# A graph-attention layer: most of the output stage placed between the last edge steps, joined rows loaded in one piece, and a node stage with paired statistics and half its rows on GpSimd

## Chip, core and metric

The kernel runs on one core of a Trainium2 chip. The core has a matrix engine (PE, with a separate record of its weight loads, PEld), a vector engine (DVE), an activation engine (ACT), GpSimd (POOL) and SyncE (SP); SP, ACT and POOL also issue DMAs, and 16 DMA engines move the bytes. The metric is the device time of one execution in microseconds (us).

## What is computed

12,500 nodes with 128 features and 400,000 edges, sorted by target node:

```python
h = jnp.maximum(_layernorm(x), 0.0)
msg = (h @ w_src + b_src)[src] + (h @ w_dst)[dst]        # per edge
msg = msg * edge_weight1 * radial_mlp(edge_attr_32)
msg_h = (msg @ w_sep + b_sep).reshape(E, 8, 32)          # 8 heads
alpha, value = smooth_leaky_relu(msg_h[:, :, :16]), msg_h[:, :, 16:]
att = segment_softmax(einsum(alpha, alpha_dot), dst)
out = segment_sum(value * att, dst).reshape(N, 128)
return x + out @ w_proj + b_proj
```

## The kernel before

**Node stage** (lines 157 to 433). The 12,500 rows are held as 98 tiles of 128 rows, worked on in 25 quads of four tiles. `stats` takes, for each tile on DVE, one batch-norm statistics and one aggregation instruction; `scales` turns them on ACT (square root) and DVE into `rstd` and `shift`; `norm` is four ACT instructions per quad (a ReLU with scale and bias); `turn` transposes the quad on PE and copies it back with DVE; `products` multiplies by `w_src` (k=0) and `w_dst` (k=1) on PE, copies with ACT, and SP stores the rows in the DRAM tables `t_src` and `t_dst`. The loop at line 407 writes the order out by hand: in turn i come the turning of quad i+1, the norm of quad i+3, the products of quad i, the statistics of quad i+5. At i=1 `load_targets` puts DMAs of single words on SP's queue; at i=6 `first` loads one block of source indices (`ri`) on SP and casts and transposes it; from i=3 on two weight loads are issued per turn; at i=13 `fits` computes `bad`, which picks this path or a fallback. `cuts` (line 361) comes last.

**Edge stage** (`windows`, line 747). 391 steps (`NP`), each for two sections of 512 edges. `gather` (line 856) issues 128-row indirect DMAs of `t_src` on POOL, eight per step. The values of a section are summed per target by `values`, `one_hot` and `sums`, 13 steps later (`LAG`), so that after the last gather 14 more steps drain (the loop at line 1353, j = 0 to 13). Each step's sums `ob` (three buffers) go by `store_win` to `win` and by `store` (line 1083) as two 63-row DMAs on SP to the rows of `agg` at an address read from a register. A section's first and last node are shared with its neighbours; those rows are joined in 13 blocks, whose results stand in `obs_d`, and `scatter` (line 1190) writes each block to `agg` with an indirect DMA on POOL. Before, the drain's step j loads one block into `comb` (two buffers, line 1359) and scatters it; a `store` of step c >= 384 is declared independent of the scatters, one below is not. The last two blocks are computed in the drain itself (`jobs`, lines 1341 to 1368).

**Output stage** (`final`, line 1387), after the drain. It loads `agg` in nine pieces of up to 12 tiles on SP (line 1396), divides by the softmax's sums (`quotients`, DVE), and then for each of 25 quads: `turn` (PE, copy on ACT), `finish` (product with `w_proj` on PE, addition of `x_fin` on DVE, store of `out` on SP, line 1434). `x_fin` is loaded on ACT in the drain. All of these tiles have 128 partitions, but for the last of 84 rows.

**Rows of 125.** One transfer of the kernel before has tiles of 125 partitions: `zero` (line 136) writes `z` (125 partitions of 680 values) over `agg`, 20 times, two per step, at the start of the edge stage.

Of the kernel before, what the change touches and what calls it, by code (L numbers as in the profile page):

```python
# [21 lines left out]
F32 = mybir.dt.float32  # L22
# [8 lines left out]
P = 128  # L31
C = 128
# [24 lines left out]
def gnn_kernel(ctx: ExitStack, tc: tile.TileContext, a: dict, out: bass.AP):  # L57
# [9 lines left out]
    NX = -(-NP // MP) * MP * PR  # L67
    assert NT * P == E and RC * RP == E and NT % TPI == 0 and NT % SORT_T == 0
# [88 lines left out]
    with tc.tile_pool(name="node", bufs=2) as np_, tc.tile_pool(name="node1", bufs=1) as n1, \  # L157
# [6 lines left out]
        for t0, t1 in groups:  # L164
            nc.sync.dma_start(out=x_all[:, t0:t1, :], in_=x_v[:, t0:t1, :])
        nc.sync.dma_start(out=x_all[:tail, NF, :], in_=x[NF * P:, :])
# [12 lines left out]
        ends = n1.tile([NH, 17, 2], I32, name="ends")  # L179
        eb = n1.tile([P, NS, 2], I32, name="eb")  # L180
# [6 lines left out]
        def load_targets():  # L187
# [3 lines left out]
            with nc.allow_non_contiguous_dma(reason="single targets"):  # L191
                nc.sync.dma_start(out=cur[1:P, 0:1], in_=bass.AP(at.tensor, at.offset, [[CC, P - 1], [1, 1]]))
                at = dst[0:1]
                h = NH - 1
                nc.sync.dma_start(out=ends[0:h], in_=bass.AP(
                    at.tensor, at.offset, [[34 * SEC // 2, h], [SEC, 17], [SEC - 1, 2]]))
# [28 lines left out]
        mv = n1.tile([P, NB, 2], F32, name="mv")  # L225
        nc.vector.memset(mv, 1.0)
# [3 lines left out]
        def stats(t0, t1):  # L230
            for t in range(t0, t1):
                n = rows(t)
                st = np_.tile([P, nc.vector.BN_STATS_DIM], F32, name="st", bufs=4)
                nc.vector.bn_stats(st[:n], x_all[:n, t, :])
                nc.vector.bn_aggr(mv[:n, t, :], st[:n])

        def scales(t0, t1):
            s = slice(t0, t1)
            nc.scalar.activation(rstd[:, s], mv[:, s, 1], AF.Sqrt, bias=eps, scale=1.0)
            nc.vector.reciprocal(rstd[:, s], rstd[:, s])  # L240
            nc.vector.scalar_tensor_tensor(shift[:, s], mv[:, s, 0], -1.0, rstd[:, s],
                                           op0=ALU.mult, op1=ALU.mult)

        def norm(i):
            t0, t1 = quads[i]
            hs[i] = np_.tile([P, 4, C], F32, name="h", bufs=4)
            for t in range(t0, t1):
                n = rows(t)
                nc.scalar.activation(hs[i][:n, t - t0, :], x_all[:n, t, :], AF.Relu,
                                     bias=shift[:n, t:t + 1], scale=rstd[:n, t:t + 1])  # L250

        def turn(i):
# [3 lines left out]
            for t in range(t0, t1):  # L256
# [3 lines left out]
            nc.vector.tensor_copy(x_all[:, t0:t1, :].rearrange("p u n -> p (u n)")[:, :w],  # L260
                                  pt.rearrange("p u n -> p (u n)")[:, :w])
# [44 lines left out]
        def fits():  # L306
# [14 lines left out]
            nc.vector.tensor_copy(bad, sum_)  # L321
# [425 lines left out]
    def windows():  # L747
# [7 lines left out]
        with tc.tile_pool(name="ps", bufs=1, space=PSUM) as pp, \  # L755
# [327 lines left out]
            def store(c, f):  # L1083
                at = nc.sync.value_load(base[0:1, f, c:c + 1])
                st = nc.sync.dma_start(out=agg[ds(at, W - 1), :], in_=accs[c][f * W:(f + 1) * W - 1, :])
                if 2 * c + 1 >= (NC - 1) * (P // 2):
                    tc.declare_no_dep(st.ins, group="combined", reason="its rows follow those of the blocks")
# [102 lines left out]
            def scatter(g):  # L1190
# [6 lines left out]
                tc.add_to_no_dep_group("combined", st.ins)  # L1197

            comb = {}

            def combined(g):
                comb[g] = tail_pool.tile([P, ROW], F32, name="comb", bufs=2)
                return comb[g]
# [128 lines left out]
            tail_pool = held.enter_context(tc.tile_pool(name="fin1", bufs=1, side="right"))  # L1332
            x_fin = tail_pool.tile([P, NB, C], F32, name="x_fin")
            x_loads = load_xb(x_fin)
            last = NC - 1

            def out_rows(g):
                block_rows_out(g, combined(g))
# [13 lines left out]
            assert SB * (NC - 1) + LAG + 1 == NP + 7  # L1352
            for k in range(NP, NP + LAG + 1):
# [9 lines left out]
            for _ in x_loads:  # L1363
                pass
# [5 lines left out]
            with tc.tile_pool(name="fin", bufs=3) as fp:  # L1370
                final(fp, x_fin, lambda i: pp.tile([P, 4, P], F32, name=("pm0", "pm1", "V")[i % 3]),
                      lambda i: pp.tile([P, 4, C], F32, name=("p3", "pa", "m1")[i % 3]))


    XQ = 12
    out_v = out[0:NF * P, :].rearrange("(p t) c -> p t c", t=NF)
    agg_v = agg[0:NF * P, :].rearrange("(p t) c -> p t c", t=NF)

    def load_xb(x_fin):

        for t0, t1 in groups:
            nc.scalar.dma_start(out=x_fin[:, t0:t1, :], in_=xb_v[:, t0:t1, :])
            yield
        nc.scalar.dma_start(out=x_fin[:tail, NF, :], in_=xb[NF * P:N, :])
        yield

    def final(fp, x_fin, turned, product):
        starts = list(range(0, NB, XQ))
        gs, qs, qTs = {}, {}, {}

        def load_g(i):

            gs[i] = fp.tile([P, XQ, ROW], F32, name="g", bufs=len(starts))
            for n, t0, t1 in blocks(starts[i], min(starts[i] + XQ, NB)):
                o = starts[i]
                nc.sync.dma_start(out=gs[i][:n, t0 - o:t1 - o, :],
                                  in_=agg_v[:, t0:t1, :] if n == P else agg[NF * P:N, :].unsqueeze(1))

        def quotients(i):
            r = fp.tile([P, XQ, H], F32, name="r")  # L1400
            qs[i] = fp.tile([P, XQ, C], F32, name="q")
            g = gs.pop(i)
            for n, t0, t1 in blocks(starts[i], min(starts[i] + XQ, NB)):
                s = slice(t0 - starts[i], t1 - starts[i])
                m = t1 - t0
                nc.vector.tensor_scalar(r[:n, s, :], g[:n, s, C:ROW], 1e-16, None, op0=ALU.add)  # L1406
                nc.vector.reciprocal(r[:n, s, :], r[:n, s, :])  # L1407
                nc.vector.tensor_mul(  # L1408
                    qs[i][:n, s, :].rearrange("p t (h k) -> p (t h) k", h=H),
                    g[:n, s, 0:C].rearrange("p t (h k) -> p t h k", h=H),  # L1410
                    r[:n, s, :].unsqueeze(3).to_broadcast([n, m, H, C // H]))

        def turn(i):
            t0, t1 = quads[i]
            q, o = qs[t0 // XQ], t0 // XQ * XQ
            pt = turned(i)
            for t in range(t0, t1):
                n = rows(t)
                nc.tensor.transpose(pt[:, t - t0, :n], q[:n, t - o, :], ident[:n, :n])  # L1419
            w = (t1 - t0 - 1) * P + rows(t1 - 1)  # L1420
            qTs[i] = fp.tile([P, 4, P], F32, name="qT")
            nc.scalar.copy(qTs[i].rearrange("p u n -> p (u n)")[:, :w], pt.rearrange("p u n -> p (u n)")[:, :w])

        def finish(i):
            t0, t1 = quads[i]
            qT = qTs.pop(i)
            py = product(i)
            for t in range(t0, t1):
                n = rows(t)
                nc.tensor.matmul(py[:n, t - t0, :], qT[:, t - t0, :n], w_proj, start=True, stop=True)  # L1430
            for n, u0, u1 in blocks(t0, t1):
                y = x_fin[:n, u0:u1, :]
                nc.vector.tensor_add(y, py[:n, u0 - t0:u1 - t0, :], y)  # L1433
                nc.sync.dma_start(out=out_v[:, u0:u1, :] if n == P else out[NF * P:N, :].unsqueeze(1), in_=y)

        for i in range(len(starts)):
            load_g(i)
        quotients(0)
        turn(0)
        for i in range(Q):  # L1440
            if i % 3 == 1 and i // 3 + 1 < len(starts):
                quotients(i // 3 + 1)
            if i + 1 < Q:
                turn(i + 1)
            finish(i)


# [3 lines left out]
    with fit.Else():  # L1451
# [23 lines left out]
        with tc.tile_pool(name="fin_b", bufs=3) as fp, tc.tile_pool(name="fin1_b", bufs=1) as f1, \  # L1475
                tc.tile_pool(name="fin_ps", bufs=2, space=PSUM) as fps, tc.manual_schedule():
            x_fin = f1.tile([P, NB, C], F32, name="x_fin")
            for _ in load_xb(x_fin):
                pass
            final(fp, x_fin, lambda i: fps.tile([P, 4, P], F32, name="pt"),  # L1480
                  lambda i: fps.tile([P, 4, C], F32, name="py"))
# [36 lines left out]
```

## Time and profile before

| | us |
|---|---|
| median of three runs (lowest, highest) | 4234.25 (4232.47, 4238.16) |
| the profiled execution | 4228.57 |
| its span | 4226.8 |
| first gather starts / last one ends | 99.45 / 4030.71 |
| first and last scatter of a block start | 4086.34 / 4153.97 |
| first load of `agg` issued / last addition ends | 4156.12 / 4220.05 |

| stretch, us | PE busy | DVE | ACT | POOL | granted PE clock | DMA share |
|---|---|---|---|---|---|---|
| 40 to 60 | 15.44 | 13.32 | 12.18 | 0.00 | 0.82 | 0.42 |
| 60 to 80 | 16.16 | 16.52 | 16.46 | 0.00 | 1.00 | 0.60 |
| 300 to 320 | 20.00 | 15.46 | 9.30 | 15.12 | 1.00 | 0.70 |
| 4100 to 4120 | 8.62 | 5.18 | 0.68 | 1.94 | 0.60 | 0.28 |
| 4180 to 4200 | 13.27 | 13.95 | 5.27 | 0.00 | 0.98 | 0.30 |

The first table is the execution from outside; the span is the part that the trace covers. The second gives each engine's busy time in a stretch of 20 us; the DMA share is the mean busy share of the 16 DMA engines.

### The profile page before, as it was taken

The page shows a single profiled execution, that of the slowest core. Times are in us where ns is not written, and L with a number is a line of the kernel's source. Part 1 is how long each engine was busy: PE and PEld are TensorE (multiplying, and loading weights), DVE is VectorE, ACT ScalarE, POOL GpSimd, SP SyncE. Part 2 cuts the span into 40 slices and gives each one's busy share as a digit, 9 for nine tenths or more (in the row PEclk, how much of TensorE's full clock was granted, in tenths as well). Part 3 has the DMA queues.
Part 4 walks back from the last instruction along what each step waited for, and adds up shares of the span by engine and source line. Part 5 has one row for each costly group of instructions (what it writes and reads, how often), then busy time and mean ns, then how long its engine had stood idle before and what let it go on. Part 6 is the DMA issues. An engine that isn't in the chain of part 4 may idle for free. (4 is left out here: it accounts for less than half of the span.)

```text
span 4226.8 us, 87991 instructions
## 1 busy us (share of the span) xinstructions
PE 3921.2 (93%) x29351; PEld 2394.1 (57%) x29351; DVE 3124.1 (74%) x6334; ACT 1919.2 (45%) x4597; POOL 2987.1 (71%) x3147
## 2 busy tenths in 40 slices
PE   6779999999999999999999999999999999999975
PEld 5345555555555555555555555555555555555554
DVE  6567777777777777777777777777777777777754
ACT  6344444444444444444444444444444444444421
POOL 0777777777777777777777777777777777777710
PEclk9889999999999999999999999999999999999988
DMA  6766776676776776676676676666766766666634
GB/s 217 218 193 178 189 195 178 195 194 185 189 198 188 187 194 187 182 195 189 186 193 194 183 192 179 179 184 185 187 183 180 189 180 183 188 178 185 184 86 160
DMA packets 593333, 783.08 MB, mean 185 GB/s; under 512 B 125553, under 2 KB 392302, under 8 KB 592740
## 3 DMA queue, kind: packets, MB, share of 16 engines
q1 hardware_dynamic: 384786, 514.16, 40.0%
q0 software_dynamic: 100416, 205.44, 22.2%
q10 hardware_dynamic: 107666, 57.76, 4.6%
q8 instruction: 234, 3.83, 0.4%
q14 instruction: 231, 1.89, 0.2%
HBM read 637.83 MB, written 139.30 MB: 184 GB/s over the span
## 5 line engine op out<-in xcount | busy, mean ns | idle before, releaser
L862 POOL DMA_INDIRECT gs<-t_src,idx x3125 | 2972.9, 951 | 1055.6 <-issue 802.6
L951 ACT ACTIVATE sl<-pa,c_b_a 128x512 f32<-128x512 f32 x782 | 536.9, 687 | 1021.1 <-PE pa L949 1006.6
L956 DVE SCALAR_TENSOR_TENSOR al<-pa,sl 128x512 f32<-128x512 f32 x782 | 540.4, 691 | 594.2 <-ACT sl L951 571.3
L1060 PEld LDWEIGHTS V<-c_w_v,mT 128*128 128x128 f32 x6048 | 746.6, 194 | 292.2 <-DVE ob L1077 122.3
L1060 PE MATMUL V<-c_w_v,mT 128*128 128x128 f32 x6048 | 879.1, 289 | 0.0
L949 PE MATMUL pa<-mT,c_w_a 128*128 128x512 f32 x1564 | 814.6, 603 | 3.5 <-DVE mT L943 2.6
L1062 DVE TENSOR_TENSOR pvx<-V,Pem 128x512 f32<-128x512 f32 x756 | 519.0, 687 | 243.7 <-PE V L1060 231.9
L929 PEld LDWEIGHTS pm<-ident,gs 128*128 128x128 f32 x3125 | 393.6, 142 | 421.3 <-issue 338.4
L1073 PEld LDWEIGHTS misc<-pvx,oh 128*64 128x64 f32 x6250 | 353.8, 138 | 408.4 <-ACT h L885 395.2
L921 DVE SCALAR_TENSOR_TENSOR rad<-p,c_fc_b,w_b 128x512 f32<-128x512 f32 x782 | 550.2, 745 | 39.5 <-PE p L913 4.3
L1073 PE MATMUL misc<-pvx,oh 128*64 128x136 f32 x6250 | 455.6, 288 | 116.1 <-ACT h L885 108.5
L943 DVE SCALAR_TENSOR_TENSOR mT<-pm,c_b_src,rad 128x512 f32<-128x512 f32 x782 | 550.7, 746 | 3.1 <-PE pm L936 3.1
L899 ACT ACTIVATE h<-p,b 128x512 f32<-128x512 f32 x391 | 287.5, 735 | 420.0 <-PE p L896 380.9
L929 PE MATMUL pm<-ident,gs 128*128 128x128 f32 x3125 | 472.3, 274 | 0.2 <-DMA gs<-t_src,idx 0.2
L913 PE MATMUL p<-h,w3b 64*128 64x512 f32 x1564 | 405.8, 596 | 12.5 <-ACT h L899 12.5
L936 PE MATMUL pm<-ohT,m 64*128 64x512 bf16 x2346 | 322.4, 381 | 0.0
L982 ACT ACTIVATE Sp<-m,b_s 128x512 f32<-128x512 f32 x192 | 131.9, 687 | 394.2 <-PE m L965 394.2
L881 PE MATMUL m<-eT,w1b 64*128 64x256 f32 x782 | 274.5, 431 | 27.6 <-DVE M L1003 18.1
L881 PE MATMUL misc<-eT,w1b 64*128 64x256 f32 x782 | 274.4, 431 | 0.0
L1046 DVE TENSOR_TENSOR oh<-lane,misc 128x504 f32<-128x504 f32 x391 | 262.2, 671 | 0.1
L896 PE MATMUL p<-h,w2b 64*64 64x256 f32 x3128 | 259.8, 402 | 0.6 <-DVE rad L921 0.6
L949 PEld LDWEIGHTS pa<-mT,c_w_a 128*128 128x128 f32 x1564 | 241.7, 195 | 20.7 <-DVE mT L943 6.2
(172 smaller groups left out, 3680.4 us busy)
## 6 DMA issues: line engine op xcount, KB each, us to landing
w_b<-in_edge_weight SPq DMA_DIRECT2D x390, 512.0 KB
d_b<-in_dst SPq DMA_DIRECT2D x390, 256.0 KB
gs<-t_src,idx POOLq DMA_INDIRECT x3125
e_t<-in_edge_attr ACTq DMA_DIRECT2D x390, 128.0 KB
sc_d<-Sp SPq DMA_DIRECT2D x192, 256.0 KB
win<-ob SPq DMA_DIRECT2D x391, 68.0 KB
agg<-ob SPq DMA_DIRECT2D x782, 33.5 KB
md<-t_dst SPq DMA_DIRECT2D x782, 32.0 KB
```

Of the source, the lines that this page charges most:

```text
L862: nc.gpsimd.indirect_dma_start(out=gs[:, t, :], out_offset=None, in_=t_src[:, :], in_offset=bass.IndirectOffsetOnAxis(ap=idx[:, t0 + t:t0 ...
L881: nc.tensor.matmul(p1[q], w1b[s, :], eTs[k][s, :], start=True, stop=True)
L913: nc.tensor.matmul(p3s[k][:, f, 0:SEC], w3b[s, :], h2s[k][s, :], start=True, stop=True)
L921: nc.vector.scalar_tensor_tensor(rad[:, s], p3[:, f, 0:n], b3, w_g[k][:, s], op0=ALU.add, op1=ALU.mult)
L929: nc.tensor.matmul(pms[k, f][:, t * T:(t + 1) * T], gs[:, t, :], ident, start=(t == 0), stop=False, is_transpose=True, skip_group_check=True)
L943: nc.vector.scalar_tensor_tensor(mTs[k][:, s], pms.pop((k, f))[:, 0:n], b_n, rad[:, s], op0=ALU.add, op1=ALU.mult)
L949: nc.tensor.matmul(pa[:, 0:n], w_a, mTs[k][:, f * SEC:f * SEC + n], start=True, stop=True)
L951: nc.scalar.activation(sl[:, 0:n], pa[:, 0:n], AF.Silu, bias=b_a, scale=1.0)
L956: nc.vector.scalar_tensor_tensor(al, pa, 0.25, sl, op0=ALU.mult, op1=ALU.add)
L1060: nc.tensor.matmul(V[:, t, :], mTs[c][:, o:o + T], w_v, start=True, stop=True)
L1062: nc.vector.tensor_mul(pvx[c][:, f, 0:n, 0:C].rearrange("p t (h k) -> p t h k", h=H), V[:, 0:n, :].rearrange("p t (h k) -> p t h k", h=H), ...
L1073: nc.tensor.matmul(acc[f * W:(f + 1) * W, :], ohs[c][:, f * TS + t, :], pvx[c][:, f, t, :], start=(t == 0), stop=(t == n - 1), skip_group_ ...
```

## The change

Four things. (1) `stats`: one statistics instruction reads two tiles interleaved, 256 values, and its two halves are the two tiles' statistics; there is no aggregation. (2) `norm`: two rows of tiles of a quad stay on ACT, two go to POOL; the ReLU moves into DVE's copy in `turn`. `load_targets` gets one more single-word DMA, for a check that joins `bad`. (3) The 11 blocks whose joined rows stand ready are loaded in one DMA at the start of the drain and scattered at once; these scatters are declared independent of the stores of steps c >= 352, whose rows follow theirs. (4) The output stage is cut into 25 units of 500 nodes, held as 125 partitions of four rows. Units 0 to 19 are run in the drain, two per step from j=4 on, with loads on ACT (`x` eight buffers, `agg` nine) and stores on SP; the last five come after the last scatter.

```diff
         def stats(t0, t1):
-            for t in range(t0, t1):
...
-                nc.vector.bn_stats(st[:n], x_all[:n, t, :])
-                nc.vector.bn_aggr(mv[:n, t, :], st[:n])
+            for t in range(t0, t1, 2):
+                nc.vector.bn_stats(mv[:, t:t + 2, :].rearrange("p u v -> p (u v)"),
+                                   x_all[:, t:t + 2, :].rearrange("p u c -> p c u"))
...
-                nc.scalar.activation(hs[i][:n, t - t0, :], x_all[:n, t, :], AF.Relu,
-                                     bias=shift[:n, t:t + 1], scale=rstd[:n, t:t + 1])
+                if t - t0 < 4 - 2:
+                    nc.scalar.activation(hs[i][:n, t - t0, :], x_all[:n, t, :], AF.Identity,
+                                         bias=shift[:n, t:t + 1], scale=rstd[:n, t:t + 1])
+                else:
+                    nc.gpsimd.tensor_scalar(hs[i][:n, t - t0, :], x_all[:n, t, :], rstd[:n, t:t + 1],
+                                            shift[:n, t:t + 1], op0=ALU.mult, op1=ALU.add)
...
             def store(c, f):
...
-                if 2 * c + 1 >= (NC - 1) * (P // 2):
-                    tc.declare_no_dep(st.ins, group="combined", reason="its rows follow those of the blocks")
+                if 2 * c >= EARLY_S:
+                    tc.declare_no_dep(st.ins, group="early", reason="its rows follow those of the early blocks")
+                    tc.add_to_no_dep_group("later", st.ins)
...
+            ready = fin.tile([P, last - 1, ROW], F32, name="ready", bufs=1)
+            nc.sync.dma_start(out=ready, in_=obs_d[0:(last - 1) * P, :].rearrange("(g p) c -> p g c", p=P))
+            for g in range(last - 1):
+                comb[g] = ready[:, g, :]
+                scatter(g)
+            un = Units(fin, 8, 9, lambda u: pp.tile([P, 4, P], F32, name=("V", "pa")[u % 2]),
+                       lambda u: pp.tile([P, 4, C], F32, name=("p3", "m1")[u % 2]))
+            un.load_x(0, 7)
...
             for k in range(NP, NP + LAG + 1):
                 step(k)
                 j = k - NP
                 if j in jobs:
                     jobs[j]()
-                if 0 <= j - 2 < NC - 2:
-                    nc.sync.dma_start(out=combined(j - 2), in_=obs_d[(j - 2) * P:(j - 1) * P, :])
-                    scatter(j - 2)
-                if j >= 3:
-                    next(x_loads, None)
...
+                if j == 3:
+                    for u in range(7):
+                        un.load_g(u)
+                    un.quotients(0)
+                    un.quotients(1)
+                    un.turn(0)
+                if j >= 4:
+                    un.run(2 if j < 12 else 1, EARLY)
             block_rows(last)
+            un.run(1, EARLY)
             block_columns(last)
+            un.run(1, EARLY)
             block_totals(last)
             out_rows(last)
+            un.run(NU, EARLY)
+            un.close(EARLY)
             work.close()
...
+            un.open(EARLY, NU)
+            un.run(NU, NU)
+            un.close(NU)
...
+    UP, UT = 125, 4
+    UN = UP * UT
...
+        def view(self, t, u):
+            return t[u * UN:(u + 1) * UN, :].rearrange("(p t) c -> p t c", t=UT)
...
+                    self.x[u] = self.pool.tile([UP, UT, C], F32, name="xu", bufs=self.nx)
+                    nc.scalar.dma_start(out=self.x[u], in_=self.view(xb, u))
...
+            self.g[u] = self.pool.tile([UP, UT, ROW], F32, name="g", bufs=self.ng)
+            eng = nc.scalar if u < EARLY else nc.sync
+            ld = eng.dma_start(out=self.g[u], in_=self.view(agg, u))
...
+        def finish(self, u):
+            qT, py, y = self.qT.pop(u), self.product(u), self.x.pop(u)
+            for t in range(UT):
+                nc.tensor.matmul(py[:UP, t, :], qT[:, t, :], w_proj, start=True, stop=True)
+            nc.vector.tensor_add(y, py[:UP], y)
+            nc.sync.dma_start(out=self.view(out, u), in_=y)
...
+        def run(self, n, end):
+            for _ in range(n):
+                if self.nf >= end:
+                    return
+                u = self.nf
+                v = max(self.g, default=u) + 1
+                if v < end:
+                    self.load_g(v)
+                while self.nq < min(u + 3, end):
+                    self.quotients(self.nq)
+                while self.nt < min(u + 2, end):
+                    self.turn(self.nt)
+                self.finish(u)
+                self.load_x(u + 7, u + 8)
```

More of the change, by code (lines that the diff above doesn't have):

```diff
@@ L67, in gnn_kernel @@
     NX = -(-NP // MP) * MP * PR
+    NU = 25
+    EARLY = 20
+    EARLY_S = (-(-2 * NS // P) - 2) * (P // 2)
     assert NT * P == E and RC * RP == E and NT % TPI == 0 and NT % SORT_T == 0
@@ L165, in gnn_kernel @@
             nc.sync.dma_start(out=x_all[:, t0:t1, :], in_=x_v[:, t0:t1, :])
+        nc.vector.memset(x_all[:, NF, :], 0.0)
         nc.sync.dma_start(out=x_all[:tail, NF, :], in_=x[NF * P:, :])
@@ L179, in gnn_kernel @@
         ends = n1.tile([NH, 17, 2], I32, name="ends")
+        lim = n1.tile([1, 1], I32, name="lim")
         eb = n1.tile([P, NS, 2], I32, name="eb")
@@ L192, in load_targets @@
                 nc.sync.dma_start(out=cur[1:P, 0:1], in_=bass.AP(at.tensor, at.offset, [[CC, P - 1], [1, 1]]))
+                at = dst[EARLY_S * SEC:EARLY_S * SEC + 1]
+                nc.sync.dma_start(out=lim, in_=at.unsqueeze(1))
                 at = dst[0:1]
@@ L222, in weights_list @@
             return [lambda t=t, ap=ap: nc.sync.dma_start(out=t, in_=ap) for t, ap in pairs]
-        mv = n1.tile([P, NB, 2], F32, name="mv")
-        nc.vector.memset(mv, 1.0)
+        mv = n1.tile([P, NB, 3], F32, name="mv")
+        assert NB % 2 == 0
         rstd = n1.tile([P, NB], F32, name="rstd")
@@ L1197, in scatter @@
                 tc.add_to_no_dep_group("combined", st.ins)
+                if g < NC - 2:
+                    tc.declare_no_dep(st.ins, group="later", reason="its rows precede those of the later sections")
+                    tc.add_to_no_dep_group("early", st.ins)
+                else:
+                    tc.declare_no_dep(st.ins, group="early", reason="its rows follow those of the early units")
+                    tc.add_to_no_dep_group("later", st.ins)
             comb = {}
-            def combined(g):
-                comb[g] = tail_pool.tile([P, ROW], F32, name="comb", bufs=2)
-                return comb[g]
             stages = {0: lambda g: (block_load(g), block_rows(g)), 2: block_maxima, 4: block_factors,
@@ L1329, in windows @@
             held.close()
-            tail_pool = held.enter_context(tc.tile_pool(name="fin1", bufs=1, side="right"))
-            x_fin = tail_pool.tile([P, NB, C], F32, name="x_fin")
-            x_loads = load_xb(x_fin)
+            fin = held.enter_context(tc.tile_pool(name="fin", bufs=2, side="right"))
             last = NC - 1
+            ready = fin.tile([P, last - 1, ROW], F32, name="ready", bufs=1)
[6 more added lines that the diff above has]
+            un.load_x(0, 7)
             def out_rows(g):
-                block_rows_out(g, combined(g))
+                comb[g] = fin.tile([P, ROW], F32, name="comb")
+                block_rows_out(g, comb[g])
                 scatter(g)
@@ L1351, in windows @@
             }
-            assert SB * (NC - 1) + LAG + 1 == NP + 7
+            assert SB * (NC - 1) + LAG + 1 == NP + 7 and EARLY == 20
             for k in range(NP, NP + LAG + 1):
@@ L1375, in gnn_kernel @@
[L1375 to L1445, printed above, removed]
@@ L1474, in gnn_kernel @@
               ea_s.rearrange("(t p) c -> p t c", p=P), "b")
[L1475 to L1481, printed above, removed]
+        with tc.tile_pool(name="fin_b", bufs=3) as fp, tc.tile_pool(name="fin_ps", bufs=2, space=PSUM) as fps, \
+                tc.manual_schedule():
+            un = Units(fp, 10, 10, lambda u: fps.tile([P, 4, P], F32, name="pt"),
+                       lambda u: fps.tile([P, 4, C], F32, name="py"))
+            un.load_x(0, 7)
+            for u in range(7):
+                un.load_g(u)
+            un.run(NU, NU)
 def kernel(**inputs):
```

55 lines of the change are left out of this document (43 added, 12 removed).

## The prediction

> **What bounds the kernel now.** I read the page first, then the timeline of both ends, the table by stretches, what SP waited for, and the DMA view of short windows. On the page I want the engine that paces the long middle.
>
> ```profile
> span 4226.8 us, 87991 instructions
> L862 POOL DMA_INDIRECT gs<-t_src,idx x3125 | 2972.9, 951 | 1055.6 <-issue 802.6
> ```
>
> 3125 gathers of 0.951 us with 0.30 us of issue behind each make 3909 us; the first starts at 99.45 and the last ends at 4030.71, 3931 us apart. So POOL runs through almost without a gap: what moves the first gather moves everything behind it, one to one. Before it lies the node stage (99 us), behind it the drain (4031 to 4154) and the output stage (4156 to 4220), then 6.7 us to the end of the span.
>
> In the node stage I look for what stands still. In the timeline (start, duration, engine, operation, idle before and what ended it):
>
> ```profile
> 25.44 6.44 SPq L195 DMA_DIRECT2D ends<-in_dst  x1
> ...
> 40.77 0.43 SPq L292 DMA_DIRECT2D ri<-in_src  x1
> ...
> 42.75 0.23 DVE L294 CAST rows<-ri 128x128 f32<-128x128 int32 x1 [4.38 <-DMA ri<-in_src]
> ```
>
> DVE, and PE behind it, wait for `ri`, which SP issues late: from 24.24, when the ACT copy of quad 1 lets the second `t_src` store go, SP issues without a pause.
>
> In the drain SP waits (in total, times, longest):
>
> ```profile
> SPq L1085 <- DMA agg<-comb,ids: 20.6, 4, 11.4
> SPq L1085 <- DMA agg<-ob: 12.2, 17, 3.5
> ```
>
> Stores and scatters of `agg` take turns; SP's steps are 6.7 us apart (`comb` loads at 4095.86, 4102.53, 4110.32, 4116.73) where PE alone had done 3.1 (L1060 at 4084.34, 4087.93, 4091.01).
>
> Last, how many DMA engines a transfer uses, since the change turns tiles of 128 partitions into 125. While `zero`'s 125-row stores are almost alone (195.6 to 196.2), and in the output stage's loads of 128 rows (4160 to 4174; the last two columns are DMA share and GB/s):
>
> ```profile
> q1 hardware_dynamic: 27, 0.07, 30.5%
> ```
> ```profile
> 4160.00:4174.00 14.00, 8.10 (x55) 7.70 (x56) 7.44 (x10) 2.93 (x5) 0.00 (x0) 0.74 1.01 404
> ```
>
> SP's queue keeps 30.5% of 16 engines busy, 4.9 of them, with two such stores in flight; loads of 128 rows keep all 16. The trace's packet records say the same: five chains of 2720-byte packets, 108 ns each, back to back. The last store, of 84 rows, shows 98 packets on that queue:
>
> ```profile
> q1 hardware_dynamic: 98, 0.04, 10.9%
> ```
>
> 84 rows and 14 small closing packets; a 63-row store has 63 and 9. Fourteen, nine and five are the largest divisors up to 16 of 84, 63 and 125.
>
> **Node stage.** Statistics of a quad take DVE four times 0.395 us (L234 and L235, from start to start); two instructions of 256 values replace them. No row shows one: bounds are 0.26 us each (no longer than 128 values) and 0.52 (twice), and I take 0.40, near the 1.04 ns a value by which L1408 grows from 128 values (0.29) to 1536 (1.76). That saves 0.8 us a quad. The two rows left on ACT save it 0.82 us (0.41 each). POOL's rows have no row either: from 0.28 (the 128x128 select on POOL) to 0.95 (a gather); I take the first, and two a quad stay below 2.3 us even with the last. DVE's copy with maximum replaces one of the same shape: 0.69, nothing. The new memset of one tile (0.17, as L112) and two single-word DVE operations in `fits` lie under the wait for the first rows (until 6.03) and under PE: nothing, or 0.5 us if DVE were late there.
> - Up to the stall: the ACT copy at 23.65 hangs on the statistics of five quads (4.0) and one halved norm (0.8); behind it SP's issues are fixed, plus 0.4 for the new word. The stall ends 4.4 earlier.
> - Behind it: the last turn starts at 90.44, 47.3 after the stall, for 17 periods. PE's own period is 2.22 us (49.56, 51.78, 54.00), and ACT needs 2.28 (two rows 0.82, two copies 1.04, half of 0.30 and of the 0.53 wait). 17 times 2.28, 1.5 for `fits` and 1.3 for the first cold products make 41.6: 5.7 saved. PE's last 56 products (6.4) stay.
>
> Sum: 10 us, between 4 (slow statistics) and 12.
>
> **Output stage and drain.** By engines alone the change looks large. A unit costs DVE 1.9 us (0.24 + 0.38 + 0.65 for the quotients, scaled from L1406 to L1408, and 0.65 for the addition) and PE 1.33 (L1419 and L1430); a drain step costs DVE 2.2 and PE 3.2. Two units in a step make 6.0 on DVE, some 6.8 with waits; from 4084, when the first loads have landed, eight such steps, two short ones and the last block would put the last scatter near 4158, and five units behind it end the span at 4180 instead of 4226.8. SP's 20.6 us go in any case; late is then what feeds the units.
>
> By DMA it looks different. Packets of 2048 bytes take 86 ns in the records (L1434's stores), 2176 bytes some 90, between those and the 108 of 2720. On five engines each takes 25 packets in a row: `x` 2.15 us, `agg` 2.25, `out` 2.15, so 6.55 us a unit and 164 us for 25; on 16 engines it would be 51. Other transfers of the drain on the same engines (28 stores of 63 rows at 0.2, 14 of 128 at 0.25, scatters) add 7. Whether ACT's and SP's queues use the same five, the trace does not show: two stores from one queue do, which is the nearest row, and I take that. Then the first seven `x` loads start at 4058.5 (ACT is free at 4057, the step loop's tiles are released with the last message, 4058.5) and end by 4073.5; the `agg` loads wait for ACT until 4081.7 (its place behind the transposed softmax), about 10 us of empty engines; from there they are full. 4058.5 + 164 + 7 + 10 is 4239.5 for the last packet; from last packet to the span's end was 3.7 before (4223.1 to 4226.8): 4243, which is 16 us later. DVE and PE, with 3.6 us a unit, hide behind the 6.55.
>
> The moved steps beside that: the joined rows come in one SP issue (0.4) at the start of the drain instead of eleven, and the eleven early scatters take POOL 11 times 1.25 = 14 us from about 4061, done before the first `agg` load is issued at 4081.7; nothing, or 1 us per scatter that is late. Stores of the last three steps now wait for the scatter of block 11, from which they were exempt; behind them on SP stand `win` and `out` stores, for which the next sums and the `x` buffers wait. A scatter's round trip was 2.2 us (4098.42 to the store at 4100.63): hidden while the five engines have a backlog, 2 us without it.
>
> On the two queues the Trainium skill speaks, on the page DMA: Bandwidth & Descriptors, section "Why a DMA increments its semaphore by 16 and not by 1": DMAs from SP and ACT go to the lowest-numbered engines, as many as the largest number up to 16 that divides both sides' slowest dimension. By that both queues share the five, and the sum stays 16 us later; the counts 14, 9 and 5 above agree, and no row here shows which engines.
>
> **Sum.** -10 and +16: the span grows by 6 to 7 us. The profiled execution took 4228.57 (span and 1.8 around it); the median of the runs is 5.7 above. I put the same shift on the median: 4234.25 + 6.5, about **4241 us**. Own range: node between 4 and 12, packets 2 to 3% slower (their neighbours' share) or the idle time 5 shorter: 4228 to 4250.
>
> **Rivals.**
> - **All 16 engines** carry the units: `agg` loads of 816 KB in the output stage did. Against: 125 rows never did here. Span end 4180 and the node's 10: 57 less, 4177.
> - **Two queues, two sets of five.** Loads then take 4.4 us a unit, stores run beside them: from 4082, 20 `agg` and 13 `x` loads put unit 19 near 4160, its scatter at 4168, five loads (2 + 11), a unit and the end near 4194. -32 and -10: 4192. For it: nothing shows ACT's engines; against: nothing shows any other choice either.
> - **Slower: SP's own order.** A store to `agg` waits for the one before it (12.2 us above); now the `out` stores of the step before stand ahead of it in SP's queue, on the same engines. ACT waits for them too, since from unit 1 on an `x` load needs the buffer that the `out` store of eight units before frees; behind that wait on ACT are the copies of the next unit and the next step's weights, which PE needs. Each step SP can stand still for two stores, 4.3 us. That costs nothing while ACT's queue holds loads, and its whole length when ACT's queue runs dry: it decides when less than two loads are waiting there. From 1.5 to 3 us in eight steps: 12 to 24 more, 4253 to 4265, most likely 4258.
> - **The exemptions free nothing:** stores and scatters still take turns, and the units only fill the gaps that they leave; the end stays where it was, and the node's 10 go: 4224. Against: the early scatters lie 20 us ahead of the stores that waited for them. Inside the range, and in the 0.05 below.
>
> **Chances.** The forecast 0.55, SP's order 0.15, two sets 0.15, all engines 0.10, other 0.05. About 0.2% (8.5 us) is what a measurement of this kernel can tell from no change. The forecast's own range reaches over that bound above (0.20 of its 0.55) and hardly below (0.03). Faster: 0.03 + 0.15 + 0.10. Slower: 0.20 + 0.15. Same: the rest, 0.37. The range leaves out all engines and little else: 4190 to 4264.
>
> **What would show it.** The first gather near 89.5 (right: node). Between 4083 and the end, a DMA share near 0.3 and 125 GB/s without gaps, units 6.5 us apart, the last scatter near 4200, the chain of waits full of DMA. Wrong: a share of 0.6 and more with units 3 to 4 us apart (more engines), or gaps in the share while SP waits for `agg` (the slower rival); a gather that starts at 97 would mean that the stall at `ri` did not move.

## Result: 0.6% slower

| | before | after |
|---|---|---|
| median of four runs each (lowest, highest), us | 4233.36 (4232.17, 4238.16) | 4262.07 (4259.70, 4262.55) |
| ratio, with its 95% interval | | 1.0064 (1.005 to 1.0078) |
| the profiled execution / its span | 4228.57 / 4226.8 | 4261.91 / 4260.1 |
| first gather starts | 99.45 | 85.12 |
| last gather ends | 4030.71 | 4020.98 |
| from there: first unit load of `agg` issued | | 66.9 later |
| last scatter starts | 123.3 later | 207.7 later |
| end of the span | 196.1 later | 239.1 later |

So 9.7 us arrive from the node stage, and 43.0 are lost behind the last gather; 33.3 is the growth of the span. In what follows, **the tail** is the stretch from the last gather's end to the end of the span, and times in the drain are told from that gather. Beside the first eight experiments below the kernel before took 5330 to 5333 us and beside the last four 4235 to 4237, so each is compared with the before measured beside it, by ratio and by tail.

### The profile page after: what moved, and what is told of

Its sections match the earlier page's. It is cut to its first block, busy times and chain, and to the rows that moved or that the text cites. A ratio compares the mean times of both kernels' runs of the same rounds, so it can differ in the third digit from the quotient of the medians.

```text
span 4260.1 us, 87963 instructions
## 1 busy us (share of the span) xinstructions
PE 3929.5 (92%) x29357; PEld 2402.9 (56%) x29357; DVE 3112.6 (73%) x6232; ACT 1900.3 (45%) x4549; POOL 3012.3 (71%) x3195
## 5 line engine op out<-in xcount | busy, mean ns | idle before, releaser
L960 PE MATMUL pa<-mT,c_w_a 128*128 128x512 f32 x1564 | 815.6, 604 | 14.3 <-DVE al L967 11.0
```

The lines of the kernel that those rows point to most:

```text
L960: nc.tensor.matmul(pa[:, 0:n], w_a, mTs[k][:, f * SEC:f * SEC + n], start=True, stop=True)
```

## The profile after

The middle is as before. From the page of the changed kernel (busy us, mean ns, idle before):

```profile
span 4260.1 us, 87963 instructions
...
L873 POOL DMA_INDIRECT gs<-t_src,idx x3125 | 2974.0, 952 | 972.8 <-issue 805.0
```

The node stage, groups of the stretch up to 85 us with shapes kept apart: rows on POOL, rows on ACT, the paired statistics.

```profile
L258 POOL TENSOR_SCALAR h<-x_all,rstd,shift 128x128 f32<-128x128 f32 x48 | 23.7, 507 | 48.2 <-PE pm L278 29.2 <-DVE shift L246 11.1 <-DVE part L126 5.5
L255 ACT ACTIVATE h<-x_all,shift,rstd 128x128 f32<-128x128 f32 x49 | 21.6, 487 | 7.4 <-DVE shift L246 6.9 <-DVE span L319 0.6
L239 DVE BATCH_NORM_STATS2 mv<-x_all 128x6 f32<-128x256 f32 x49 | 18.4, 419 | 4.6 <-DMA x_all<-in_x 4.6
```

A statistics instruction of 256 values takes 0.42 us, a row on POOL 0.51. The timeline at the stall and at the first gather:

```profile
35.67 0.43 SPq L301 DMA_DIRECT2D ri<-in_src  x1
...
37.69 0.23 DVE L303 CAST rows<-ri 128x128 f32<-128x128 int32 x1 [9.38 <-DMA ri<-in_src]
```
```profile
85.12 1.18 POOL L873 DMA_INDIRECT gs<-t_src,idx  x1 [10.99 <-DMA t_src<-ms]
```

`ri` is issued at 35.67 instead of 40.77, and the stall ends at 37.69 instead of 42.75. The wait before the cast reads 9.38 instead of 4.38, and still the stall ends earlier: DVE got there sooner.

In the drain, the table by stretches (busy PE, PEld, DVE, ACT, POOL; granted clock; DMA share; GB/s):

```profile
4080.00:4100.00 20.00, 10.42 (x65) 8.79 (x65) 9.67 (x23) 2.83 (x10) 0.00 (x0) 0.67 0.23 72
4100.00:4120.00 20.00, 12.35 (x97) 11.49 (x96) 11.05 (x25) 2.64 (x6) 0.00 (x0) 0.84 0.36 135
4160.00:4180.00 20.00, 15.86 (x124) 14.27 (x122) 13.34 (x31) 2.07 (x5) 0.00 (x0) 0.87 0.36 129
4200.00:4220.00 20.00, 7.29 (x52) 6.46 (x48) 5.71 (x14) 1.96 (x5) 0.00 (x0) 0.83 0.32 92
4220.00:4240.00 20.00, 4.25 (x17) 3.10 (x17) 3.09 (x10) 0.74 (x3) 0.91 (x1) 0.50 0.23 81
4240.00:4260.00 20.00, 8.25 (x56) 7.73 (x56) 7.46 (x15) 2.69 (x5) 0.00 (x0) 0.76 0.30 102
```

The share stands still at 0.35 to 0.36 and some 130 GB/s while the early units run, and sinks from 4200 on. The DMA view of 4100 to 4200 splits it by queue (packets, MB, share of 16 engines):

```profile
q1 hardware_dynamic: 4482, 4.75, 13.6%
q10 hardware_dynamic: 3974, 8.09, 21.6%
```

SP's queue (q1) and ACT's (q10) together keep 35.2% of 16 engines busy, 5.6. Without the small stores, the packets of the units alone (2048 and 2176 bytes, both queues) are five at a time for 70 of these 100 us, six for 16 (records overlap at their ends), and 4.9 on the mean. That is one set of five engines for both queues, and it is full. The `out` stores go out two by two, one pair a step; from the first pair to the eighth are 94.7 us (4106.81 to 4201.54), 14 units of 6.8 us.

Ahead of that the five are not full. ACT's timeline there (start, duration of the group of issues, idle before):

```profile
4047.58 14.01 ACTq L1419 DMA_DIRECT2D xu<-xb  x7
4061.64 0.34 ACT L1051 COPY pvx<-Pem 128x32 f32<-128x32 f32 x2 [14.26 <-DMA xu<-xb]
...
4083.60 0.63 ACT L1026 ACTIVATE Pr<-M 128x512 f32<-128x512 f32 x1 [14.96 <-DVE M L1024]
...
4087.93 7.76 ACTq L1424 DMA_DIRECT2D g<-agg  x7
```

Seven loads of `x` hold ACT for 14 us, though an issue that does not wait takes 0.26; then ACT waits 15 us for the maxima of the last softmax, and only at 4087.93 does it come to the `agg` loads. The end of the chain of waits that ended last:

```profile
4228.70 3.63 DMA agg<-comb,ids
...
4232.77 6.60 DMA g<-agg
...
4241.86 1.71 PE p L1449 x8
...
4249.92 0.69 DVE xu L1450
```

The last scatter, the five loads behind it, five units: 31 us in a row. From 4200 on the five engines have gaps. Counted as packet time of the units that is missing against the 4.92 at a time of 4100 to 4200, they lack 6.9 us before the last scatter (4200 to 4228.7) and 2.5 us between it and the first packets of the loads behind it (4228.7 to 4233.3). From there to 4257 they are full again, with 5.0 packets at a time: the shares of 0.30 to 0.32 are mostly these five engines without the small stores. SP's and ACT's timelines at the first gap:

```profile
4196.69 4.80 SPq L1096 DMA_DIRECT2D agg<-ob  x2
4201.54 0.70 SPq L1451 DMA_DIRECT2D out<-xu  x2
...
4206.22 0.34 ACT L1051 COPY pvx<-Pem 128x32 f32<-128x32 f32 x2 [8.99 <-DMA out<-xu]
```

SP stands at two stores to `agg` and issues the `out` stores behind them only at 4201.54; ACT waits 9 us for an `out` store to free an `x` buffer; and from 4200.91 to 4202.34 no unit's packet runs at all.

## The experiments

In the first eight (first condition in the table) the whole middle is slower: in runs 1 to 4, 710 to 725 gathers start more than 1.5 us after the one before, where before's own profile has 24; from 1000 to 1100 us PE is busy 81.6 us at a granted clock of 0.95 in run 1, and 96.7 us at 1.00 in before's own profile. What causes it stays open. The tail is 4 to 7 us longer there: before's drain and output stage take 201.0 (run 1) instead of 196.1, the change's 243.1 (run 2) instead of 236.3 to 239.1.

| run | ratio to before (95%) | `agg` loads issued | last scatter | tail, us |
|---|---|---|---|---|
| *first condition* | | | | |
| node stage alone | 0.9975 (0.9958 to 0.9992) | | 129.6 | 201.0 |
| tail alone | 1.0089 (1.0055 to 1.0123) | 72.6 | 212.2 | 243.1 |
| cut transfers | 0.9945 (0.9926 to 0.9965) | 69.7 | 160.9 | 184.8 |
| `x` loads spread | 1.0055 (1.0037 to 1.0072) | 72.0 | 211.3 | 242.8 |
| cut and spread | 0.9947 (0.9924 to 0.9969) | 70.7 | 158.9 | 183.3 |
| one unit a step | 1.0080 (1.0057 to 1.0103) | 75.2 | 180.2 | 255.6 |
| `out` on GpSimd | 1.0006 (0.9982 to 1.0029) | 73.8 | 190.2 | 222.8 |
| cut, all units last | 0.9979 (0.9953 to 1.0005) | | 114.2 | 200.5 |
| *second condition* | | | | |
| the change itself | 1.0050 (1.0033 to 1.0066) | 65.0 | 205.8 | 236.3 |
| cut, `out` on GpSimd | 0.9918 (0.9901 to 0.9934) | 58.4 | 148.5 | 178.0 |
| cut, `x` and `out` on GpSimd | 0.9920 (0.9903 to 0.9936) | 58.4 | 151.3 | 183.1 |
| as the run two lines up, one unit a step | 0.9943 (0.9929 to 0.9956) | 55.3 | 136.8 | 183.0 |

**1. The node stage alone.** The kernel before with the new `stats`, `scales`, `norm` and `turn`:

```diff
-                nc.vector.bn_stats(st[:n], x_all[:n, t, :])
-                nc.vector.bn_aggr(mv[:n, t, :], st[:n])
+                nc.vector.bn_stats(mv[:, t:t + 2, :].rearrange("p u v -> p (u v)"),
+                                   x_all[:, t:t + 2, :].rearrange("p u c -> p c u"))
...
+                    nc.gpsimd.tensor_scalar(hs[i][:n, t - t0, :], x_all[:n, t, :], rstd[:n, t:t + 1],
+                                            shift[:n, t:t + 1], op0=ALU.mult, op1=ALU.add)
```

> The kernel before with the node stage of the changed kernel alone (paired statistics, half the rows on GpSimd); drain and output stage as before. Theory, the gathers carry the node's gain to the end: the first gather starts near 85 instead of 99.5, the last ends near 4021 instead of 4030.7, and the time is 4233.4 - 9.7, about 4224 (4219 to 4227). Rival, the drain gives it back (its start is not set by the last gather): 4233, no change.

The first gather starts at 83.64; the time is 0.25% shorter (14 us of 5330), with an interval that reaches from 4 to 22 us. The gain goes through. The last gather ends at 5094.5, so the absolute times that were expected do not apply, here and in the next runs.

**2. The rest alone.** The changed kernel with before's node stage (the same diff backwards).

> The changed kernel with the node stage of before: joined rows, early scatters and the 25 units stay. Theory, the two parts add: the drain and output part alone costs about 38 us, and the time is 4262.1 + 9.7, about 4272 (4267 to 4277). Rival, the two parts meet in the drain (the end is set by something that the last gather does not move): 4262.

0.89% slower, 47 us (the interval reaches from 29 to 66), with a tail of 243.1, 42.1 longer than run 1's; the whole change has 43.0. The product of the two ratios, 1.0064, is the ratio of the whole change: within these intervals the parts add.

**3. The transfers cut so that they divide.**

```diff
+    CUT = ((0, 112), (112, UP))
...
-                    nc.scalar.dma_start(out=self.x[u], in_=self.view(xb, u))
+                    for p0, p1 in CUT:
+                        nc.scalar.dma_start(out=self.x[u][p0:p1], in_=self.view(xb, u)[p0:p1])
```

and the same for the `agg` load and the `out` store.

> The changed kernel, with each transfer of a unit cut into rows 0 to 111 and rows 112 to 124, so that its rows divide among 16 and 13 engines. Nothing else moves. Theory, five engines pace the units and through SP's and ACT's queues the steps: a unit's three transfers take 3 times 8 packets in a row instead of 3 times 25, 2.1 us instead of 6.5; ACT is no longer held 14 us by the first seven loads; the time is 4175 to 4200. Rival, SP's order (each store to agg waits for the one before it, with two out stores ahead): the waits stay, shorter by the transfers alone, and the time stays above 4235.

The tail falls from 243 (runs 2 and 4) to 184.8. The same bytes in more DMAs take 58 us less, and the kernel is 0.55% faster than before. The expected 4175 to 4200 stood for 62 to 87 us less than 4262: the theory's cause holds, its size was a little too large. A stretch of the drain:

```profile
5220.00:5240.00 20.00, 15.22 (x122) 13.50 (x122) 14.03 (x37) 4.43 (x14) 0.00 (x0) 0.91 0.72 211
```

The DMA share is 0.72 instead of 0.36, and PE and DVE work 15 and 14 of 20 us. SP's order was left as it was; the rival is out as the main cause.

**4. The first seven `x` loads spread,** transfers whole.

```diff
-            un.load_x(0, 7)
...
+                if j < 4:
+                    un.load_x(2 * j, min(2 * j + 2, 7))
```

> The changed kernel, with the first seven loads of joined x rows issued two a step over the last steps instead of all seven at once ahead of them. Theory, ACT's stand of 14 us on these issues (4047.6 to 4061.6) holds the last steps and all behind them: 4248 to 4254. Rival, five engines are the bound whatever the order: the time stays within 4 us of 4262.

The tail is 242.8, not shorter: the theory on ACT's stand fails. ACT's timeline says where the 14 us went:

```profile
5171.38 0.63 ACT L1026 ACTIVATE Pr<-M 128x512 f32<-128x512 f32 x1 [18.95 <-DVE M L1024]
...
5179.70 8.35 ACTq L1425 DMA_DIRECT2D g<-agg  x7
```

ACT now arrives early and waits 19 us for the last softmax's maxima, and the `agg` loads are issued at 72.0, as in run 2 (72.6). In SP's queue the six `S<-Sp` stores of that softmax take 9.78 us to issue, in run 2 3.77; now they run beside the `x` loads, which is the likely reason and was not tried by itself.

**5. Cut and spread together.**

```diff
+    CUT = ((0, 112), (112, UP))
...
+                if j < 4:
+                    un.load_x(2 * j, min(2 * j + 2, 7))
```

> The cut transfers (rows 0 to 111 and 112 to 124) and, as well, the first seven loads of joined x rows issued two a step. Theory: once the engines are free, ACT's stand on those loads (9.5 us in the run with cut transfers alone) holds the last steps, and the stretch from the last gather to the end of the span shrinks from 184.8 to about 175. Rival: the same loads then meet the stores and loads of the last softmax, as they did with whole transfers, and the stretch stays within 3 us of 184.8.

183.3 against 184.8: within the rival's 3 us. ACT's stand is not on the path with short transfers either.

**6. One unit between the steps instead of two,** 12 early units, 13 behind the last scatter, transfers whole.

```diff
-    EARLY = 20
+    EARLY = 12
...
-                    un.run(2 if j < 12 else 1, EARLY)
+                    un.run(1, EARLY)
...
-            un.open(EARLY, NU)
+            un.open(EARLY, min(EARLY + 7, NU))
```

> The changed kernel with one unit instead of two between the last steps, 12 early units instead of 20, and 13 behind the last scatter; whole transfers on five engines. Theory, the five engines are the bound and the order only places them: the last scatter comes 50 us or more earlier than 207 us after the last gather, yet the stretch from the last gather to the end of the span stays at 235 to 245. Rival, SP's order (out stores ahead of the stores to agg, ACT's waits for out stores) costs 12 us or more by itself: the stretch falls under 228.

Both missed. The last scatter comes 32 us earlier, not 50, and the tail is 255.6, 12 to 13 more. While the steps run (5215 to 5295) the share is 0.33, with the units' packets on 0.81 of five engines; behind the last scatter (5305 to 5360) they fill them. A step with a single unit took some 8 us (nine from 5206 to 5281), more than the unit's 6.8 of transfers. ACT's waits between 5190 and the end (total, times, longest):

```profile
ACT qT L1443 <- DMA out<-xu: 41.0, 5, 11.6
ACT pvx L1051 <- DMA out<-xu: 35.4, 6, 8.8
```

These are the waits of an `x` load for the `out` store that frees its buffer, with the step's copies behind it. Here, where too little is queued, the engines run empty beside them, as the slower rival described; how much of the loss these waits make was not tried by itself.

**7. The `out` stores on GpSimd,** transfers whole.

```diff
-            nc.sync.dma_start(out=self.view(out, u), in_=y)
+            nc.gpsimd.dma_start(out=self.view(out, u), in_=y)
```

> The changed kernel with the out stores of the units issued by GpSimd instead of SP. Theory, five engines: if GpSimd's queue uses the same engines the stretch from the last gather to the end of the span stays at 235 to 245; if it uses others, a unit needs 4.4 us instead of 6.5 on the five, and the stretch is near 200. Rival, SP's order: the five engines stay full of loads and stores (97 to 101% as now), and still the last scatter comes 12 to 24 us earlier because no out store stands ahead of a store to agg.

222.8, between the cases. GpSimd's queue uses more than the five engines. The timeline of POOL and the DMA view of 5204 to 5207, in which two such stores run:

```profile
5202.98 0.61 POOL L1451 DMA_DIRECT2D out<-xu  x1 [30.61 <-DVE r L1432]
5204.78 0.55 POOL L1451 DMA_DIRECT2D out<-xu  x1 [1.20 <-DVE xu L1450]
```
```profile
q0 software_dynamic: 107, 0.36, 45.5%
```

45.5% of 16 are 7.3 engines on the mean of these 3 us, for 125 rows. The packets of the loads then fill 0.85 of the five (5200 to 5270), where loads and stores in run 2 fill 0.98 (5200 to 5290), so the five are no longer the whole bound, and the last scatter comes 22 us earlier than in run 2. How much of it is the order and how much the load on the five, this run does not separate.

**8. All units behind the last scatter,** transfers cut; the first seven `x` loads stay ahead.

```diff
-    EARLY = 20
+    EARLY = 0
...
-                if j >= 4:
-                    un.run(2 if j < 12 else 1, EARLY)
...
+            un.open(0, 7)
```

> The cut transfers with no unit between the steps: joined rows and early scatters stay, all 25 units follow the last scatter. Theory, the interleaving pays once transfers are short: the drain alone ends in its last scatter near 110 us after the last gather, 25 units of 2.2 to 2.6 us follow, and the stretch is 175 to 195, no better than 184.8 with units between the steps. Rival, the interleaving itself costs (steps and units wait for each other on ACT and SP): under 172.

200.5, above the theory's upper end. The drain alone has its last scatter at 114.2, and 25 units take 86 us, 3.4 each, not 2.2 to 2.6, with a DMA share of 0.72 to 0.80 from 5240 to 5300. Against run 3 the interleaving is worth 16 us once transfers are short.

**9. Cut loads, `out` on GpSimd** (the diffs of runs 3 and 7 together).

> The cut transfers for the loads of the units, and their out stores issued by GpSimd instead of SP. With the engines free, this tells what SP's order costs by itself: in the run with cut transfers SP spent 19 us in the drain waiting at stores to agg with out stores ahead of it in its queue. Theory, the transfers were the bound and SP's order hides behind PE and DVE: the stretch from the last gather to the end of the span stays within 4 us of 184.8. Rival, SP's order: 12 us or more go, the stretch is 173 or less.

178.0 in the second condition; 184.8 less the 4 to 7 us between the conditions is 178 to 181. With that correction the theory holds; cut transfers with the stores on SP were not run in the second condition. No `out` store stands ahead of a store to `agg` any more, and SP waits at them all the same (4085 to the end):

```profile
SPq L1096 <- DMA agg<-ob: 15.4, 11, 2.9
```

**10. `x` on GpSimd too,** ahead of the early scatters, and five units of `agg` ahead instead of seven.

```diff
-                    nc.scalar.dma_start(out=self.x[u], in_=self.view(xb, u))
+                    nc.gpsimd.dma_start(out=self.x[u], in_=self.view(xb, u))
```

> As the run before it, with the loads of joined x rows on GpSimd as well (the first seven ahead of the early scatters) and five instead of seven joined aggregate rows' units loaded ahead: ACT issues the cut loads of agg alone. Theory: ACT's two stands (9.5 us at the seven x loads, 8.2 us at the seven agg loads in the run with cut transfers) held the steps; with them shortened the stretch is 165 to 176 and the time 1% below the kernel before. Rival, GpSimd's queue fills and its scatters come late: the stretch is no better than 184.8.

ACT's stand at the `x` loads is gone, and the tail is 183.1, no better: the theory's 165 to 176 was missed. The rival's reason is not seen either, since the early scatters start 32.7 us after the last gather (run 9: 34.5). The `agg` loads are issued at 58.4 as in run 9: ACT waits 16.68 us for the softmax's maxima instead. The time equals run 9's.

**11. The change itself again.**

> The changed kernel itself beside the others, for a common measure. Theory, node and tail add: its ratio to the kernel before is the product of the two parts alone, 0.9975 x 1.0089 = 1.0064, and the stretch from the last gather to the end of the span is 239 to 244. Rival, the slower middle of this chip changes the drain too: a ratio outside 1.004 to 1.009.

1.0050 (1.0033 to 1.0066), tail 236.3, some 3 below the expected range. The ratio agrees with the sum of the parts.

**12. Run 9 with one unit a step.**

```diff
-                    un.run(2 if j < 12 else 1, EARLY)
+                    un.run(1, EARLY)
```

> The run with cut loads and out stores on GpSimd, with one unit instead of two between the last steps; the early units that are left over follow the last scatter's issue and fill the time until the rows behind it can be loaded (from 4160 to 4185 PE was busy 10 of 20 us there). Theory: with short transfers a step with one unit is some 2 us shorter, the last scatter comes 10 to 16 us earlier than 148.5 us after the last gather, and the stretch to the end of the span falls from 178.0 to 164 to 172; the time is 1 to 1.2% below the kernel before. Rival, the units only change places: 176 to 182.

The last scatter comes 12 us earlier, as the theory said, but the tail is 183.0, one above the rival's 176 to 182: the units change places, and the time is 0.6% below before, not 1 to 1.2%. SP's timeline shows one reason:

```profile
4157.40 11.17 SPq L1427 DMA_DIRECT2D g<-agg  x10
```

The ten issues for the last five units take 11.2 us instead of 4.1 in run 9: SP waits there for `x` loads and for other `agg` loads of the units still open.

**The better version.** Runs 9 and 10 beat both kernels: 0.9918 (0.9901 to 0.9934) of before, where the change is at 1.0050 beside them.

## Why the prediction came out as it did

4241 was forecast, 4262 measured. The sign was on the forecast's side, as was its main cause; its own range (4228 to 4250) missed by 12. The wide range of the last line (4190 to 4264) holds the time by 2 us only because it was drawn around rivals as well. The time lies where the slower rival put it (4253 to 4265), and in the main not for the rival's reason. Both of these are luck.

- **Gathers pass the node's gain on.** 14.3 us at the first gather are 9.7 at the last. 2.3 are gone by gather 125, where one stall (5.97 us behind PE's product at L883) is 3.4 longer than before; the rest is a few longer gaps along the way. "One to one" was too simple, by 4.6.
- **Node stage, -10.** Mechanism right, size too small: 14.3. The stall ends 5.1 earlier (forecast 4.4). Behind it PE runs at its own period of 2.22 us (L267 at 42.29, 44.51, 46.74), not at ACT's 2.28: 40.6 from the stall to the last turn (78.31 - 37.69) in place of 47.8 (90.55 - 42.75), so 7.2 saved and not 5.7. The remaining 2.1 lie between PE's last product and the gather; why they went is open. The 0.42 for the statistics stood at 0.40 in the sum; POOL's 0.51 at 0.28, and being beside other work it cost nothing.
- **Five engines, 6.55 us a unit and 7 for others.** Right: 6.8 us a unit with the others in it. Run 3 shows that this is the bound: 58 us go when the rows divide, and runs 4 and 5 show that ACT's stand on the `x` loads is not what went. The Trainium skill, DMA: Bandwidth & Descriptors, section "Why a DMA increments its semaphore by 16 and not by 1", has both queues on the same lowest-numbered engines; the 5.6 engines for the two queues together agree, and the "two sets of five" are out.
- **"About 10 us of empty engines" ahead of the `agg` loads.** This step failed. Packets of `x` run from 4048.5 to 4068.3 and the `agg` loads are issued at 4087.93, 20 us later. Against the last gather they are issued at 66.9 where the forecast had 51.0 (4081.7 - 4030.7): 16 late. The forecast priced the seven `x` loads by their transfers on idle engines and saw no one behind them. Behind them stood ACT, and with it the last steps and the last softmax. Spreading the loads (run 4) brought nothing: the `agg` loads are issued at 72.0 instead of 72.6, behind a longer wait for the softmax's maxima. In run 10, with the `x` loads on GpSimd, they are issued at 58.4, still 7 behind the forecast's 51.0; why is open.
- **"From there they are full."** This held from 4089 to 4200 (4.9 packets of the units at a time) and from 4233 to 4257 (5.0), and failed between: some 10 us are missing there, 6.9 of them ahead of the last scatter, which started at 4228.7 and not near 4200. Up to 4220 it is SP's and ACT's waits at `agg` and `out` stores that stand beside the gaps (3.8 us missing); then the last block's rows are loaded and computed with no unit beside them, and the loads of the last five units wait for the scatter. The transfers themselves were nearly right: from the first `agg` load on, the units' packets add up to 156.8 us of five engines, where the forecast had 149 (164 less seven `x` loads) and 7 for others. 16 late and 10 of gaps are most of the 29 by which the last packet (4258.4) missed the forecast's (4239.5 less the node's 10).
- **The slower rival, SP's own order.** Its number was right and its mechanism is in the trace: SP waits 57.4 us in 20 waits for `agg<-ob`, ACT 56.6 in 6 for `out<-xu` (from 4040 to the end):

```profile
SPq L1096 <- DMA agg<-ob: 57.4, 20, 6.9
```
```profile
ACT pvx L1051 <- DMA out<-xu: 56.6, 6, 11.1
```

  Up to 4200 they fall where the five engines are full, so they cost nothing there, as the rival's own condition says (ACT's queue was not dry). From 4200 to 4220 they stand beside 3.8 us of gaps; that is about all that can be the rival's here, of the 12 to 24 it asked for. With free engines SP's order cost nothing that could be measured (run 9, with the correction made there); with one unit a step the same waits stand beside engines that are 0.81 full (run 6).
- **Scatters and joined rows.** Right: eleven scatters from 4062.55, 1.28 apart, all issued by 4076.35, 12 us ahead of the first `agg` load.
- **All 16 engines, 4177.** Too early. Run 9 does the same work with free engines 0.8% faster than before, 35 us, where the rival had 57: by engines alone the end was put 149 us after the last gather (4180 - 4030.7), and the best tail measured is 178.

What stays open: what holds the tail at 178 to 184 in runs 3, 5, 9, 10 and 12, where neither the transfers, nor ACT's stands, nor the place of the units made a difference. No engine is full there: from 4100 to 4150 of run 9, PE and DVE are busy 40.6 and 40.8 of 50 us, at a DMA share of 0.67 to 0.75.

## What to carry to other kernels

Before a tile is recut to a handier number of rows, ask how many DMA engines its transfers will use: transfers of 125 whole rows cost this kernel 58 us of tail against the same rows cut into 112 and 13, and turned a gain into a loss. Units whose rows divide by 16 from the start were not tried. Price a burst of loads not by its bytes alone but by who is behind it, on the issuing engine and on the same DMA engines. And when work is moved ahead of a last dependence, look at what is left behind it: here five units followed the last scatter, and their transfers paid the same five engines again, 24 us at the very end.

## What the runs showed of the hardware

- **GpSimd's plain stores are cut otherwise than SP's.** The 25 stores of 125 rows of 2048 bytes show as 1550 packets of 4096 bytes and 25 of 2052 on GpSimd's queue (run 7), with 0.54 us of POOL each; alone (5303 to 5306) mostly 15 or 16 run at a time, beside the loads (5204 to 5207) mostly 11. SP's show as 125 packets of 2048, five at a time. The Trainium skill says of this in the section named above that on trn2 DMAs issued from GpSimd get 16 engines for some shapes that do not divide; the run agrees for 125 rows.
- **A queue takes a few long transfers, then its engine stands.** Of the seven `x` loads five are issued within 3.5 us, the seventh 13.8 us after the first (4061.34 - 4047.58), 7 us before the last packet of all seven.
- **Cut transfers are not 3 times as fast.** The units' packets took 113 ns each on the mean with cut transfers (run 3), 93 with whole ones (the change): with all units at the end (run 8) a unit took 3.4 us, half of 6.8.
